# A hybrid attention and feed-forward kernel on Trainium2: other shares of the dequantisation per unit, and the turn of the negated maxima behind the last scores

## The chip, the cores and the metric

The kernel runs on one core of a Trainium2 chip. The core has TensorE (matrix products into PSUM), VectorE, ScalarE and GpSimd (POOL) for work on tiles, and SyncE (SP), which here only issues DMAs. Every engine works off its own list of instructions in order; semaphores make one wait for another. The metric is the device time of one execution in microseconds (us), and less is better. Before the change it is 1792.84 us, the median of three runs (1791.84 to 1794.59).

## The reference

The input x has 2048 tokens of 256 numbers. Four layers are added to it one after the other: attention a, a feed-forward layer, attention b, and the same feed-forward layer again. Each works on a layer-normed x.

```python
x = L0_attn_a_x
x = x + _L0_attn_a_ref(_layernorm(x, axis=-1), ...)
x = x + _L0_ffn_ref(_layernorm(x, axis=-1), ...)
x = x + _L0_attn_b_ref(_layernorm(x, axis=-1), ...)
x = x + _L0_ffn_ref(_layernorm(x, axis=-1), ...)
```

Both attentions are causal, with 16 heads of 16 numbers. Attention a has biases, rotary angles and only 4 key and value heads; attention b has 16 of each and neither biases nor angles.

```python
scores = jnp.einsum('bthd,bshd->bhts', q, k) * scale
scores = jnp.where(causal[None, None, :, :], scores, -jnp.inf)
probs = jax.nn.softmax(scores, axis=-1)
attended = jnp.einsum('bhts,bshd->bthd', probs, v).reshape(B, S, hidden)
return attended @ Wo.T + bo
```

The feed-forward layer has 2048 hidden features. Its three weights come as 4-bit codes with one scale for every 32 of them, and must be dequantised; both feed-forward layers use the same weights.

```python
vals = NVFP4_LUT[idx]
vals = vals.reshape(N, K // block, block) * scales[:, :, None]
...
gelu = jnp.tanh(0.7978845608028654 * (gate + 0.044715 * gate ** 3)) * gate * 0.5 + gate * 0.5
inter = gelu * up
out = jnp.einsum('tn,hn->th', inter, Wd)
```

## The kernel before

**Blocks, groups, units.** The 2048 tokens are cut into four blocks of 512, and the 16 heads into four groups of 4. An attention stage works through 16 units (b, g), block by block, group by group. A unit computes, for 512 queries and 4 heads, the exponentials of all scores up to the diagonal and their products with the values. The number of key tiles grows with the block, so units of block 3 take some 45 to 50 us and those of block 0 some 14 to 24 us.

**What one unit holds.** The row maxima have to be known before the exponentials. So while unit n computes its exponentials, it also computes scores and row maxima of unit n + 1 (`max_steps`): TensorE multiplies (L769, with masks L757), VectorE reduces (L776). After the last of these the step `gather` (L806 to L817, five small VectorE instructions) joins the maxima, negates them and splits them into three bf16 parts in the tile m_pad. The function `turn` (L830) turns m_pad by four matmuls with an identity into a PSUM tile, and ScalarE copies that to the tile mT (L836). In the first five units' turns, four matmuls with zeros (L826) come first. The next unit begins each of its score tiles with a "lift" (L856), two matmuls that write the negated maxima out of mT into PSUM; the scores (L865) are added on top, and ScalarE takes the exponentials (L873). The products of exponentials and values (L911) add up in another PSUM tile.

**The main steps of a unit** (`value_steps`) are a list: two steps for each full key tile, then two for the diagonal squares, two for the first tile of the block, and two that hold both head pairs, `both_pairs(first + 1)` with 256 columns a pair and `both_pairs(first + 2)` with 128. A step is a tuple: its first function is issued, then the side work that falls to it, then the others. The last tuple is `both_pairs(first + 2)` and `rest(0)`, products of an earlier tile (L911 with 384 columns). The product sum is closed, divided and stored inside the first steps of the next unit (`ending`; L942 is the copy of the sum, L949 its turn, L954 and L957 the division).

**The side work of a unit** is woven evenly between the main steps (`weave`), except that the last three (blocks 1 to 3) or two (block 0) get none. It consists of the next unit's maxima, of `out_steps` (the output projection of the block before, L1007) in the first unit of a block, of `prep_steps` (layer norm, projections, rotary angles, keys and queries of the next block) in the first three units of blocks 0 to 2, and, in the first attention only, of the dequantisation. Blocks 1 and 2 put more into their third units: there the first four maxima steps for the next block are computed beside those of the unit that follows.

**The dequantisation** (`dequant_steps`) is a list of 72 steps, six for each of twelve pieces: the load of codes (SP, L330) and of scales (eight DMA issues on POOL, L339), the extraction of the lowest bytes (POOL, L344), two unpackings on VectorE (L355, L357 or L359, and L361; 128 x 128), and two scalings on VectorE (L370; 128 x 512). The load of a piece stands one piece ahead. The first eight pieces go to the gate and up weights in SBUF, the last four by way of DRAM (`wd_kept`) to the down weights. `room` (L1019) gives each unit a weight and `shares` the number of steps that are done by its end, 72 times the running sum over the whole sum, rounded up. The second attention is run with an empty list.

**Order.** All five engines' orders are written out by the program (a manual schedule): an instruction is issued on its engine where the code calls it. PSUM has three tiles ps_s for scores, maxima and the feed-forward features, one tile ps_m for turns and projections, and one ps_av for products. Four tiles hold exponentials.

**The feed-forward stage** runs over the blocks and 16 feature tiles; its first block's layer norm and turning (`beside`) lie in the last attention unit.

The lines that hand the turn to a unit's last step:

```python
if turn:
    scored, summed = steps[-1]
    steps[-1] = (turn, scored, summed)
```

Of the kernel before, what the change touches and what calls it, by code (L numbers as in the profile page):

```python
# [27 lines left out]
NG = NH // 4  # L28
# [3 lines left out]
NB = S // TB  # L32
# [10 lines left out]
def weave(main, side, rest=0):  # L43


    done = 0
    for n, step in enumerate(main):
        first, *second = step if isinstance(step, tuple) else (step,)
        first()
        want = min(len(side), -(-(n + 1) * len(side) // max(1, len(main) - rest)))  # L50
        while done < want:
            side[done]()
            done += 1
        for f in second:
            f()
    while done < len(side):
        side[done]()
        done += 1


def blend(a, b):

    keyed = [((n + 0.5) / len(a), 0, n, f) for n, f in enumerate(a)]
    keyed += [((n + 0.5) / len(b), 1, n, f) for n, f in enumerate(b)]
    return [f for *_, f in sorted(keyed, key=lambda k: k[:3])]


def cut(steps, n):

    while 0 < n < len(steps) and getattr(steps[n - 1], "open", False):  # L70
        n += 1
    return steps[:n], steps[n:]
# [8 lines left out]
def tile_hybrid_layers(  # L81
# [46 lines left out]
    def ps_m():  # L128
        return psum.tile([P, 512], F32, tag="m", name="ps_m")
# [36 lines left out]
    for src, at in ((bq, 0), (bk, D), (bv, D + 64)):  # L166
        n = src.shape[1]
# [243 lines left out]
    class Attention:  # L411
# [601 lines left out]
        def run(self, extra, beside):  # L1013


            units = [(b, g) for b in range(NB) for g in range(NG)]


            room = [0 if n < NG else 9 if n + 1 == len(units) else 2 * (g < 3 or b + 1 == NB)  # L1019
                    for n, (b, g) in enumerate(units)]  # L1020
            shares = [-(-len(extra) * sum(room[: n + 1]) // sum(room)) for n in range(len(units))]
            given, ending, ahead, early = 0, [], [], None

            def zeros():
                pt = ps_m()
                for _ in range(2):
                    nc.tensor.matmul(
                        pt, lhsT=sel[:, 0, :], rhs=nothing, start=True, stop=True
                    )

            for n, (b, g) in enumerate(units):
                lead, more = [], []
                if g == 0 and b > 0:
                    more += self.out_steps(b - 1)
                if g == 0 and b + 1 < NB:
                    ahead = self.prep_steps(b + 1)

                    third = len(ahead) / 3
                    few = [round(third) - (1 if b else 2), round(third) + (1 if b else 2) + 2 * self.first, len(ahead)]
                if g < 3 and b + 1 < NB:  # L1040
                    part, ahead = cut(ahead, few[g])
                    more += part
                if shares[n] > given:
                    more = blend(more, extra[given : shares[n]])
                    given = shares[n]
                if n == 0 and self.after:
                    lead, more = self.after[:3], self.after[3:] + more
                elif n + 2 < len(units):
                    self.load_q(*units[n + 2])
                maxima, turn = [], None  # L1050
                if n + 1 < len(units):
                    maxima, turn = early or self.max_steps(*units[n + 1])
                    early = None
                    if g == 2 and 0 < b < NB - 1:

                        others, then = self.max_steps(b + 1, 0)
                        half = len(maxima) // 2
                        maxima = maxima[:half] + blend(maxima[half:-1], others[:4]) + maxima[-1:]
                        early = others[4:], then
                else:  # L1060
                    more = blend(more, beside)
                steps, end, divide = self.value_steps(b, g)

                for at, step in zip((0, 2), ending):
                    scored, *summed = steps[at]
                    steps[at] = (scored, step, *summed)
                if turn:
                    scored, summed = steps[-1]
                    steps[-1] = (turn, scored, summed)
                if (b, g) == (0, 3):  # L1070

                    maxima = blend(maxima[:-1], [zeros] * 8) + maxima[-1:]
                some, left = (3, 3) if b else (1, 2)
                first = len(maxima) * some // len(steps)
                weave(steps[:some], lead + maxima[:first])
                weave(steps[some:], blend(maxima[first:], more) if maxima else more, rest=left)
                ending = [end, divide]
            end()
            return [divide] + self.out_steps(NB - 1)
# [93 lines left out]
    with tc.tile_pool(name="wk1", bufs=2) as wk, tc.tile_pool(name="kv1", bufs=1) as kv:  # L1173
        at.wk = at.qpool = wk
        with tc.tile_pool(name="init", bufs=1) as pool:
# [14 lines left out]
            steps, turn = at.max_steps(0, 0)  # L1190
# [16 lines left out]
    with tc.tile_pool(name="kv20", bufs=1, reuse_waits="tile") as kv0, tc.tile_pool(  # L1207
# [8 lines left out]
        steps, turn = at.max_steps(0, 0)  # L1216
# [60 lines left out]
```

## Time and profile before

| What | us |
|---|---|
| Median of three runs (lowest, highest) | 1792.84 (1791.84, 1794.59) |
| The profiled execution | 1790.76 |
| Its span, first to last instruction | 1789.0 |
| TensorE busy | 1709.7 (96%) |
| VectorE busy | 1113.2 (62%) |
| ScalarE busy | 799.8 (45%) |
| GpSimd busy | 242.2 (14%) |
| First attention, turn of unit (0,0) to the end of unit (3,3) | 36.3 to 566 |
| Second attention, likewise | 924.2 to 1446 |

All times inside an execution come from one profiled execution and are counted from the start of its span. Line numbers (L830) are those of the kernel before. In a timeline a line gives the start, the duration, the engine, the line, the operation and its tiles (written <- read), the shapes and the number of instructions merged, and in brackets how long the engine stood idle before and which instruction released it. Ends of matmuls are modelled, and neighbours on an engine overlap a little, on ScalarE and VectorE by some 0.1 us. "PEclk" is the clock that TensorE was granted, 1.00 being full. PE is TensorE, PEld its loading of weights, DVE VectorE, ACT ScalarE.

### The profile page before, as it was taken

Reading aid. Unit: us, or ns where it says so; the run is one execution under the profiler, and the core shown is the slowest. Engines: PE = TensorE matmul, PEld = TensorE weight load, DVE = VectorE, ACT = ScalarE, POOL = GpSimd, SP = SyncE. Lnnn points to the kernel's source line nnn. Section 1 sums busy time; section 2 is a strip of 40 time slices with the busy share of each in tenths; the row PEclk is TensorE's granted clock in tenths of the full one; section 3 lists DMA queues with packets and bytes.
Section 4 is the critical chain, followed back from the end, with each engine's and each line's share of the span. In section 5 each row is a group of like instructions: output and inputs, shape, how many; then the busy total and the mean of one; then the engine's idle time right before and its main releaser. Section 6 shows DMA issues by size and latency. Waiting matters only on the chain.

```text
span 1789.0 us, 30446 instructions
## 1 busy us (share of the span) xinstructions
PE 1709.7 (96%) x12814; PEld 934.3 (52%) x12829; DVE 1113.2 (62%) x1615; ACT 799.8 (45%) x1016; POOL 242.2 (14%) x476
## 2 busy tenths in 40 slices
PE   8888899899999999999998899999999999999999
PEld 4544454444443474656475445444444445565646
DVE  5667987887874626362645777777878535445352
ACT  2435556666666313131314455555666742222231
POOL 4312211201103102012101010000000001111010
PEclk9999999999999999999999999999999999999999
DMA  5321301310003000005006042032000100000000
GB/s 154 92 60 56 73 25 46 73 29 25 13 2 125 6 1 1 0 0 129 1 2 129 17 89 50 13 66 54 14 13 1 49 1 3 9 7 6 10 3 12
DMA packets 43129, 65.33 MB, mean 37 GB/s; under 512 B 14000, under 2 KB 21040, under 8 KB 42736
## 3 DMA queue, kind: packets, MB, share of 16 engines
q1 hardware_dynamic: 34352, 47.37, 9.2%
q0 software_dynamic: 7680, 15.48, 4.9%
q8 instruction: 101, 1.65, 0.4%
q10 hardware_dynamic: 960, 0.52, 0.1%
q14 instruction: 36, 0.29, 0.1%
HBM read 43.45 MB, written 17.83 MB: 34 GB/s over the span
## 4 chain that ended last, share of the span: by engine, by line
PE 57%; DVE 7%; ACT 3%; issue 1%; POOL 0%; ACTq 0%; DVEq 0%; POOLq 0%
PE ps_s L1126 24%; PE ps_m L1151 6%; PE ps_av L1151 6%; DVE mx L776 6%; PE ps_av L911 6%; PE ps_s L856 4%; PE ps_s L769 3%; PE ps_s L865 3%; ACT e L873 2%; PE ps_m L1002 1%; PE ps_m L501 1%; PE ps_s L501 1%; PE ps_s L757 1%; PE ps_m L636 0%; PE ps_m L1102 0%
## 5 line engine op out<-in xcount | busy, mean ns | idle before, releaser
L776 DVE TENSOR_REDUCE mx<-ps_s 128x2 f32<-128x1024 f32 (+3 forms) x576 | 650.2, 1160 | 198.2 <-PE ps_s L769 152.0
L873 ACT ACTIVATE e<-ps_s 128x1024 f32<-128x1024 f32 (+1 forms) x576 | 555.6, 977 | 378.4 <-PE ps_s L865 307.1
L911 PE MATMUL ps_av<-e,v 128*32 128x256 f32 (+3 forms) x4672 | 331.9, 376 | 0.1
L865 PE MATMUL ps_s<-qT,kT 64*128 64x512 f32 (+3 forms) x1664 | 329.3, 445 | 0.0
L769 PE MATMUL ps_s<-kT,qT 64*128 64x512 f32 (+3 forms) x1664 | 258.0, 364 | 30.5 <-DVE mx L776 16.2
L1126 PE MATMUL ps_s<-xnT,wg 128*128 128x512 f32 x512 | 240.9, 593 | 0.0
L1126 PE MATMUL ps_s<-xnT,wu 128*128 128x512 f32 x512 | 240.6, 592 | 0.0
L856 PE MATMUL ps_s<-mT,sel 64*128 64x512 bf16 (+3 forms) x1280 | 219.1, 354 | 19.9 <-DVE mx L776 8.4
L769 PEld LDWEIGHTS ps_s<-kT,qT 64*128 64x128 f32 x1664 | 141.8, 186 | 126.0 <-DVE mx L776 53.8
L856 PEld LDWEIGHTS <-sel 64*128 64x128 bf16 x1280 | 66.6, 93 | 230.9 <-issue 218.1
L1132 ACT ACTIVATE t<-ps_s 128x512 f32<-128x512 f32 x128 | 76.3, 596 | 244.2 <-PE ps_s L1126 243.9
L1135 ACT ACTIVATE t<-t 128x512 f32<-128x512 f32 x128 | 80.6, 629 | 198.8 <-DVE t L1134 198.8
L1134 DVE TENSOR_TENSOR t<-ps_s,t 128x512 f32<-128x512 f32 x128 | 88.1, 688 | 124.5 <-POOL t L1133 122.3
L911 PEld LDWEIGHTS ps_av<-e,v 128*32 128x32 f32 x4672 | 102.3, 109 | 113.9 <-issue 99.4
L1126 PEld LDWEIGHTS ps_s<-xnT,wu 128*128 128x128 f32 x512 | 97.3, 190 | 122.5 <-issue 122.5
L1133 POOL TENSOR_SCALAR t<-t 128x512 f32<-128x512 f32 x128 | 79.1, 618 | 534.5 <-ACT t L1132 534.0
L865 PEld LDWEIGHTS ps_s<-qT,kT 64*128 64x128 f32 x1664 | 149.2, 193 | 2.0
L1126 PEld LDWEIGHTS ps_s<-xnT,wg 128*128 128x128 f32 x512 | 95.1, 190 | 104.2 <-issue 102.5
L1136 DVE SCALAR_TENSOR_TENSOR t<-t,ps_s 128x512 f32<-128x512 f32 x128 | 88.1, 688 | 89.0 <-ACT t L1135 89.0
L1151 PE MATMUL ps_av<-wd,inter 128*128 128x256 f32 x512 | 114.4, 380 | 0.0
L1151 PE MATMUL ps_m<-wd,inter 128*128 128x256 f32 x512 | 114.1, 379 | 0.0
L1151 PEld LDWEIGHTS ps_av<-wd,inter 128*128 128x128 f32 x512 | 96.8, 190 | 16.9 <-issue 4.2
(153 smaller groups left out, 1103.5 us busy)
## 6 DMA issues: line engine op xcount, KB each, us to landing
qT<-h SPq DMA_DIRECT2D x248, 64.0 KB, 2.2
kT<-h POOLq DMA_DIRECT2D x88, 128.0 KB, 5.9
h<-high SPq DMA_DIRECT2D x24, 256.0 KB, 2.2
h<-low SPq DMA_DIRECT2D x24, 256.0 KB, 2.5
wd<-wd_kept SPq DMA_DIRECT2D x2, 2048.0 KB, 8.2
wd_kept<-dq_d SPq DMA_DIRECT2D x4, 512.0 KB, 2.7
out<-x SPq DMA_DIRECT2D x16, 128.0 KB, 1.7
x<-x SPq DMA_DIRECT2D x3, 512.0 KB, 7.7
```

What stands on the lines that cost most here:

```text
L769: nc.tensor.matmul(pt[:, r, at : at + keys.stop - keys.start], lhsT=self.qT[b, g][64 * r : 64 * r + 64, p, i * P : (i + 1) * P], rhs=self. ...
L776: nc.vector.tensor_reduce(to, pt, AX.X, ALU.max)
L856: nc.tensor.matmul(pt[:, r, at : at + queries.stop - queries.start], lhsT=sel[64 * r : 64 * r + 64, p, :], rhs=self.mT[b, g][64 * r : 64 * ...
L865: nc.tensor.matmul(pt[:, r, at : at + queries.stop - queries.start], lhsT=self.key_rows(kt // NT, g, p, r, keys), rhs=self.qT[b, g][64 * r ...
L873: nc.scalar.activation(e, pt, AF.Exp, scale=QK_SCALE)
L911: nc.tensor.matmul(held["av"][32 * j : 32 * j + 32, to], lhsT=self.vv[kt // NT][:, kt % NT, h * VW : h * VW + 32], rhs=of(j), start=openin ...
L1126: nc.tensor.matmul(pt[:, k, :], lhsT=w[:, c, fc * P : (fc + 1) * P], rhs=self.xnT[b][:, c, :], start=(c == 0), stop=(c == 1),)
L1133: nc.gpsimd.tensor_scalar(t, t, GELU_A, 1.0, ALU.mult, ALU.add)
L1134: nc.vector.tensor_tensor(t, gate, t, ALU.mult)
L1135: nc.scalar.activation(t, t, AF.Tanh, scale=GELU_C)
L1136: nc.vector.scalar_tensor_tensor(t, t, 1.0, gate, ALU.add, ALU.mult)
L1151: nc.tensor.matmul(po[:, :D], lhsT=inter[:, fc, i * P : (i + 1) * P], rhs=wd[:, fc, :], start=(fc == 0), stop=(fc == NFC - 1),)
```

## The change

The weights in `room` become a written list. The sum stays 27. In steps of the dequantisation, by unit from (0,0) to (3,3): before 0, 0, 0, 0, 6, 5, 5, 0, 6, 5, 5, 0, 6, 5, 5, 24; after 0, 0, 0, 0, 6, 5, 0, 0, 5, 8, 0, 0, 8, 6, 5, 29. The third units of blocks 1 and 2 get none, and the steps keep their order. The first attention alone has such steps.

In the last tuple of a unit, `turn` and `scored` change places, in both attentions and at all units but the last: `both_pairs(first + 2)` is issued first, then the turn with its copy on ScalarE, then `rest(0)`. On TensorE the scores of the last step (L856, L865) come ahead of L830, and on ScalarE the exponentials of that step (L873) ahead of the copy to mT (L836). The number and kind of instructions are the same on every engine. All lines behind L1018 have numbers one less.

```diff
@@ -1016,8 +1016,7 @@
             units = [(b, g) for b in range(NB) for g in range(NG)]
 
 
-            room = [0 if n < NG else 9 if n + 1 == len(units) else 2 * (g < 3 or b + 1 == NB)
-                    for n, (b, g) in enumerate(units)]
+            room = [0, 0, 0, 0, 2, 2, 0, 0, 2, 3, 0, 0, 3, 2, 2, 11]
             shares = [-(-len(extra) * sum(room[: n + 1]) // sum(room)) for n in range(len(units))]
             given, ending, ahead, early = 0, [], [], None
 
@@ -1066,7 +1065,7 @@
                     steps[at] = (scored, step, *summed)
                 if turn:
                     scored, summed = steps[-1]
-                    steps[-1] = (turn, scored, summed)
+                    steps[-1] = (scored, turn, summed)
                 if (b, g) == (0, 3):
 
                     maxima = blend(maxima[:-1], [zeros] * 8) + maxima[-1:]
```

## The prediction

> **What bounds the kernel now.** I read the page first: engine shares, then the chain that ended last.
>
> ```profile
> PE 1709.7 (96%) x12814; PEld 934.3 (52%) x12829; DVE 1113.2 (62%) x1615; ACT 799.8 (45%) x1016; POOL 242.2 (14%) x476
> ...
> PE 57%; DVE 7%; ACT 3%; issue 1%; POOL 0%; ACTq 0%; DVEq 0%; POOLq 0%
> ```
>
> TensorE is nearly always busy, so a microsecond in which it newly waits is lost, unless it would have waited later anyway. The change works in the two attention stages only (36 to 566 us and 924 to 1446 us). Next, the timeline at a boundary between two units; of thirty, fifteen look like this one, which ends unit (3,1) of the second attention. First TensorE, then ScalarE.
>
> ```profile
> 1365.90 0.48 PE L865 MATMUL ps_s<-qT,kT 64*128 64x256 f32 x4
> 1366.31 0.40 PE L830 MATMUL ps_m<-ident_b,m_pad 128*128 128x128 bf16 x4
> ...
> 1366.73 0.42 PE L865 MATMUL ps_s<-qT,kT 64*128 64x128 f32 x4
> 1367.08 0.85 PE L911 MATMUL ps_av<-e,v 128*32 128x384 f32 x8
> 1368.03 0.39 PE L856 MATMUL ps_s<-mT,sel 64*128 64x512 bf16 x2
> ```
>
> ```profile
> 1366.48 1.02 ACT L873 ACTIVATE e<-ps_s 128x1024 f32<-128x1024 f32 x1 [0.56 <-PE ps_s L865]
> 1367.40 0.58 ACT L836 CAST mT<-ps_m 128x512 bf16<-128x512 f32 x1
> 1367.86 0.62 ACT L873 ACTIVATE e<-ps_s 128x512 f32<-128x512 f32 x1
> 1368.75 1.02 ACT L873 ACTIVATE e<-ps_s 128x1024 f32<-128x1024 f32 x1 [0.27 <-PE ps_s L865]
> ```
>
> See the order: turn (L830), last scores (L865, 128 columns), their products, then the next unit's lift (L856), which needs mT. The copy of mT (L836) begins only when ScalarE has finished the exponentials of the step before (1366.48 to 1367.50), ends at 1367.98, and the lift starts 0.05 later; the products had ended at 1367.93. Copy and lift already meet there: the cover is used up.
>
> A few boundaries look otherwise, as the first one of the first attention:
>
> ```profile
> 50.09 0.23 DVE L817 TENSOR_TENSOR m_pad<-rest,m_pad 128x16 bf16<-128x16 f32 x1
> ...
> 50.38 0.40 PE L830 MATMUL ps_m<-ident_b,m_pad 128*128 128x128 bf16 x4 [2.57 <-DVE m_pad L817]
> ```
>
> Here TensorE stands 2.57 us before VectorE's last gather instruction. Last, the units by windows: (1,2), (2,1), (2,2), (3,1) of the first attention, then (3,1) of the second, which has no dequantisation.
>
> ```profile
> 173.55:203.46 29.91, 25.92 (x284) 14.21 (x285) 27.02 (x38) 16.59 (x20) 11.11 (x21) 1.00 0.35 97
> ...
> 269.63:311.17 41.54, 40.05 (x409) 20.07 (x409) 32.01 (x42) 25.88 (x31) 7.23 (x13) 1.00 0.15 48
> 311.17:352.98 41.81, 37.42 (x398) 19.25 (x397) 36.72 (x48) 24.12 (x28) 11.15 (x21) 1.00 0.24 63
> ```
>
> ```profile
> 439.62:485.07 45.45, 44.27 (x490) 20.80 (x489) 38.85 (x45) 30.61 (x32) 4.57 (x9) 1.00 0.08 24
> ```
>
> ```profile
> 1321.32:1366.31 44.99, 44.07 (x490) 21.01 (x489) 36.37 (x37) 30.60 (x32) 0.00 (x0) 1.00 0.05 13
> ```
>
> Columns: length, then busy time of PE, PEld, DVE, ACT, POOL. TensorE idles 3.99 us in (1,2) and 4.39 in (2,2), but 1.49 in (2,1) and 1.18 in (3,1): VectorE holds it up in the third units.
>
> **Part 1, the turn behind the last scores: thirty boundaries.** No instruction is added or taken. On TensorE the scores move ahead of the four turning matmuls; so ScalarE, in its own order, meets the last exponentials (0.62) before the copy (0.58). SP, POOL and VectorE keep their order. At a boundary as shown, the exponentials start where the copy did (1367.40) and the copy 0.52 later (0.62 less the 0.10 by which neighbours on ScalarE overlap). Copy ends 1368.50, lift at 1368.55 instead of 1368.03: 0.52 us. Queued behind the lift on TensorE are the next unit's scores, with them VectorE's next maxima and ScalarE's next exponentials; nothing on TensorE may pass it. Fifteen of these: 15 x 0.52 = 7.8. Four boundaries have ScalarE free earlier (copy 0.63, 0.71, 0.84 and 0.91 us after the turn's start, against 1.09): the same shift there gives 0.22, 0.29, 0.42 and 0.50, together 1.4. Stalls: 9.2.
>
> Where the gather is late, the scores fill the wait. At 50.38 the lift came 1.56 after the turn's start; afterwards only the turn and the products (0.85) precede it, about 1.12: a gain of 0.44. Four such boundaries give 0.44, 0.35, 0.44 and 0.40, one half-late one 0.11, four others (ScalarE free, gather in time) 0.2 in all, one nothing: 1.9. The thirtieth, behind (1,2), goes with part 2. Sum: +7.3. Bounds: nothing absorbed and no late gather gained, +9.2; half of each stall absorbed by the 0.48 us wait for ScalarE that follows in each such unit, +2.7. I take +7.3, because that later wait hangs on the first exponentials and so on the lift, and shifts with it.
>
> **Part 2, the shares.** Cumulative 72 x room / 27, rounded up, gave units (1,0) to (3,3) 6, 5, 5, 0, 6, 5, 5, 0, 6, 5, 5, 24 steps; it becomes 6, 5, 0, 0, 5, 8, 0, 0, 8, 6, 5, 29. The steps themselves cost the same. In (1,2) VectorE ran almost without a gap from 176 to 203 us:
>
> ```profile
> 184.14 0.89 DVE L370 SCALAR_TENSOR_TENSOR wu<-dq_e,dq_s 128x512 f32<-128x512 fp8e4 x1
> ...
> 189.01 0.67 DVE L370 SCALAR_TENSOR_TENSOR wu<-dq_e,dq_s 128x512 f32<-128x512 fp8e4 x1
> ```
>
> With overlaps taken off, these two and one unpacking step cost 0.81 + 0.59 + 0.59 = 2.0 us of its queue. TensorE's waits for VectorE there are 1.11 + 0.22 within and 1.01 at the end, so nearly all comes back at the turn: -1.9. But the exponentials before then end 0.65 after the turn's new start instead of 0.12, the last ones 0.52 later, the copy 0.47 after that: lift at 1.69 instead of 1.55, so -1.7 net. In (2,2) two unpackings and two scalings, 0.6 each, leave: of the first and third nothing is won, as VectorE waits for TensorE behind them (0.41 and 0.46 idle before its next work); of the second and fourth 0.6 each: -1.2. The bound is all 2.0 + 2.4 = -4.4 on one side, on the other the 1.01 alone, -1.0.
>
> Where the steps go: VectorE gets 1.6 us more in (2,1), 0.5 in (3,0), 0.7 in (3,2), 0.6 less in (2,0). Price: block 3 of the second attention does the same work without dequantisation; (3,0) to (3,2) are there 0.87, 0.46 and 0.93 shorter, 2.26 us for 7.28 us of dequantisation, or 0.31 per us. 2.2 x 0.31 = +0.7 (bounds 0 and 2.2). In (3,3) VectorE is busy 13.87 of 35.43 us; five more steps hide there, and the last, at 566.98, has 4.8 us before the feed-forward needs VectorE (571.80). The dequantised weights are needed later still. POOL's scale loads (eight issues, 4.0 us a piece) and SP's loads of packed codes move with the steps, behind query loads for units not yet begun: nothing, but ScalarE's copy of rotated queries in (2,1) may come late behind them, up to 1 us if that cover fails. Sum: 0.7 - 1.7 - 1.2 = -2.2.
>
> **Total** 7.3 - 2.2 = +5.1 us. The profiled execution took 1790.76 (span 1789.0 and 1.76 around it), so 1795.9; the median of three is 1792.84, which gives 1797.9.
>
> **A rule against it.** The clock shows what idling costs:
>
> ```profile
> 100.68:104.09 3.41, 1.55 (x11) 0.82 (x10) 3.38 (x5) 0.81 (x1) 0.00 (x0) 1.00 0.04 11
> 104.09:107.51 3.42, 2.88 (x11) 1.34 (x14) 1.67 (x3) 0.00 (x0) 0.00 (x0) 0.50 0.00 0
> ```
>
> After a stretch with TensorE busy 1.55 of 3.41 us the granted clock was 0.50 for the next. At the boundaries idle time grows from some 0.64 us to 1.2 in such a stretch, busy 2.2; the stretch 199.66 to 203.07, in (1,2), was as idle and 1.00 followed. By the rows: no loss. The Trainium skill (TensorE: Matmul & The Clock Gate, "A second HAM failure mode: psum-queue depth-cycling") says that frequent short idling between groups of matmuls can also make the clock oscillate. An estimate from its halved clock for one 3.4 us window at each of 19 boundaries would be 32 us more; no run here shows that.
>
> **Rivals.**
> - The stall is absorbed (other side): ScalarE's chain, not the lift, starts a unit, and the 19 stalls cost nothing. For it: the 0.48 us wait behind each. Against it: ScalarE idles 0.27 before its first exponentials, waiting for L865. Sum -1.9 - 2.2 = -4.1: 1788.7. The sign turns when a stall costs under 0.23 us.
> - Third units give back all VectorE time (-4.4, and 0 for the steps elsewhere): 7.3 - 4.4 = +2.9, 1795.7; with part of the stalls absorbed too, less. Within the bound.
> - More drops of the clock: each 3.41 us at half speed costs 1.7. Two to four: +3.4 to +6.8, 1801 to 1805. For it: early units already fall (0.50 above); against it, the busy late ones never did.
>
> **How the numbers follow.** Forecast 0.60 (own range 1795 to 1801), absorbed 0.08, all VectorE time returned 0.20, clock 0.12. A measurement tells 0.2%, 3.6 us, from no change: slower from 1796.4. The forecast's lower sixth lies below that, so slower 0.50 + 0.12, same 0.10 + 0.20, faster 0.08. All low bounds together (2.7 - 4.4 + 0) give 1791.1, all high ones (9.2 - 1.0 + 2.2 + 1) 1804.2; that all fall together is unlikely, so the range is 1792 to 1802, which leaves out the absorbed case and most of the clock's.
>
> **What would show it.** Right: the copy of mT starts 1.6 us after the last exponentials but one, the lift waits for it at late boundaries, both attention stages change, the second by about +4.0, the first by about +1. TensorE's idle falls by 1 to 2 us in (1,2) and (2,2). Wrong: the second attention, which has the turn alone, is not longer; or the granted clock falls in new places.

## The result and the profile after

The changed kernel takes 1796.71 us (median of 16 runs, 1791.84 to 1800.73), the kernel before 1791.26 us beside it (16 runs, 1789.56 to 1796.76). The ratio is 1.0030, 95% interval 1.0021 to 1.0039: 5.4 us slower (3.8 to 7.0). Differences in us against the kernel before are the ratio taken on its median, here and below; the difference of the two medians can be some 1 us off them. The profiled executions have spans of 1794.5 and 1789.0 us.

No engine does more work. The first lines of the page of the kernel after:

```profile
span 1794.5 us, 30440 instructions
## 1 busy us (share of the span) xinstructions
PE 1708.9 (95%) x12814; PEld 936.0 (52%) x12829; DVE 1112.1 (62%) x1615; ACT 799.0 (45%) x1016; POOL 242.7 (14%) x476
```

TensorE is busy 0.8 us less over a span that is 5.5 us longer: the time went into waits. The groups by line, asked for the copy to mT, tell which. Under "who waited for it (us, times)" the kernel before and then the kernel after have, for the lift (L856):

```profile
  PE ps_s L856: 1.3, 2
```

```profile
  PE ps_s L856: 15.4, 25
```

The two places before are the first units of the two attentions, and they stay. Waits of 0.10 us, as at the late boundaries before, are under what this view counts.

The boundary that the prediction showed, the end of unit (3,1) of the second attention, in the timeline of the kernel after; TensorE, then ScalarE:

```profile
1370.42 0.48 PE L865 MATMUL ps_s<-qT,kT 64*128 64x256 f32 x4
...
1370.84 0.42 PE L865 MATMUL ps_s<-qT,kT 64*128 64x128 f32 x4
1371.19 0.40 PE L830 MATMUL ps_m<-ident_b,m_pad 128*128 128x128 bf16 x4
1371.52 0.85 PE L911 MATMUL ps_av<-e,v 128*32 128x384 f32 x8
1373.05 0.39 PE L856 MATMUL ps_s<-mT,sel 64*128 64x512 bf16 x2 [0.68 <-ACT mT L836]
```

```profile
1371.01 1.51 ACT L873 ACTIVATE e<-ps_s 128x1024 f32<-128x1024 f32 x2 [0.56 <-PE ps_s L865]
1372.40 0.59 ACT L836 CAST mT<-ps_m 128x512 bf16<-128x512 f32 x1
```

The two exponentials now stand together (1.51 us), the copy starts 0.12 us before they end, and TensorE stands 0.68 us at the lift, where it stood 0.10.

For the units I take the length from lift to lift, out of the same timelines. It has the wait at the unit's end in it; for (3,3) it goes to the first matmul of the feed-forward stage.

| Stretch, us | before | after | difference |
|---|---|---|---|
| First attention, block 0 | 75.84 | 73.31 | -2.53 |
| First attention, (1,0) to (3,2) | 419.08 | 422.08 | +3.00 |
| First attention, (3,3) | 34.43 | 34.43 | 0.00 |
| Second attention, block 0 | 74.00 | 74.35 | +0.35 |
| Second attention, (1,0) to (3,2) | 413.33 | 417.75 | +4.42 |
| Second attention, (3,3) | 33.62 | 33.62 | 0.00 |
| The two feed-forward stages | 701.3 | 701.3 | 0.0 |

Block 0 is a special case. There the granted clock of TensorE falls to 0.50 for one or two stretches of 3.41 us at a time, and where this happens differs between executions (before: from 80.2 and 104.1 us of the span in the first attention; after: from 44.2 and 102.2). In the profiles of this study the first block 0 took 70.4 to 75.8 us. Nothing of the change can be read from one such number, and the other rows are the ones to compare. They add up to 7.4 us, 2.0 more than the two medians show. (What is missing to 5.5 us is the start, ahead of the first unit.)

The units of the shares, by windows of the kernel after: (1,2), (2,1), (2,2), (3,1) of the first attention.

```profile
171.35:199.80 28.45, 25.51 (x284) 14.23 (x285) 25.23 (x33) 15.88 (x20) 6.69 (x12) 1.00 0.38 86
267.18:309.22 42.04, 40.33 (x409) 20.13 (x409) 33.34 (x49) 25.97 (x32) 7.30 (x13) 1.00 0.13 41
309.22:350.83 41.61, 37.51 (x398) 18.96 (x397) 34.15 (x40) 23.89 (x28) 6.70 (x12) 1.00 0.34 72
438.77:485.27 46.50, 44.30 (x490) 21.14 (x489) 38.10 (x45) 30.59 (x33) 4.47 (x10) 1.00 0.10 30
```

VectorE lost 1.8 us of work in (1,2) and 2.6 in (2,2). TensorE's idle time fell in (1,2) from 3.99 to 2.94 us, but in (2,2) only from 4.39 to 4.10; the new stall at the lift lies within each of these. In (3,1), where VectorE has no more to do than before (38.10 against 38.85), idle time rose by 1.0, of which the stall is 0.6.

### The profile page after: what moved, and what is told of

It reads as the page before. It is cut to its first block, busy times and chain, and to the rows that moved or that the text cites. A ratio compares the mean times of both kernels' runs of the same rounds, so it can differ in the third digit from the quotient of the medians.

```text
span 1794.5 us, 30440 instructions
## 1 busy us (share of the span) xinstructions
PE 1708.9 (95%) x12814; PEld 936.0 (52%) x12829; DVE 1112.1 (62%) x1615; ACT 799.0 (45%) x1016; POOL 242.7 (14%) x476
## 4 chain that ended last, share of the span: by engine, by line
PE 74%; DVE 15%; ACT 7%; issue 2%; DMA 1%; POOL 0%; ACTq 0%; SPq 0%; DVEq 0%; POOLq 0%
PE ps_s L1125 24%; DVE mx L776 12%; PE ps_av L911 10%; PE ps_s L856 7%; PE ps_m L1150 6%; PE ps_s L769 6%; PE ps_av L1150 6%; PE ps_s L865 5%; ACT e L873 5%; PE ps_s L501 2%; PE ps_m L1002 2%; PE ps_m L501 1%; PE ps_s L757 1%; ACT mT L836 1%; PE ps_m L949 1%
## 5 line engine op out<-in xcount | busy, mean ns | idle before, releaser
L873 ACT ACTIVATE e<-ps_s 128x1024 f32<-128x1024 f32 (+1 forms) x576 | 552.1, 976 | 384.8 <-PE ps_s L865 314.1
L865 PE MATMUL ps_s<-qT,kT 64*128 64x512 f32 (+3 forms) x1664 | 327.6, 445 | 0.0
L856 PE MATMUL ps_s<-mT,sel 64*128 64x512 bf16 (+3 forms) x1280 | 219.0, 353 | 31.0 <-ACT mT L836 15.4
L856 PEld LDWEIGHTS <-sel 64*128 64x128 bf16 x1280 | 67.1, 93 | 240.1 <-issue 230.2
L865 PEld LDWEIGHTS ps_s<-qT,kT 64*128 64x128 f32 x1664 | 149.4, 193 | 1.9
```

Of the source, the lines that this page charges most:

```text
L856: nc.tensor.matmul(pt[:, r, at : at + queries.stop - queries.start], lhsT=sel[64 * r : 64 * r + 64, p, :], rhs=self.mT[b, g][64 * r : 64 * ...
L865: nc.tensor.matmul(pt[:, r, at : at + queries.stop - queries.start], lhsT=self.key_rows(kt // NT, g, p, r, keys), rhs=self.qT[b, g][64 * r ...
L873: nc.scalar.activation(e, pt, AF.Exp, scale=QK_SCALE)
```

## Experiments

The theory: the last exponentials stand ahead of the copy on ScalarE, the lift waits for the copy, and nothing later takes this up. The main rivals: it is TensorE's own order (too little left behind the turn to cover the copy), whatever ScalarE does; or the stall is taken up later; or the differences are falls of the clock. Each group of runs had its own runs of the kernel before beside it, on the same chip.

**The turn alone.** The shares of before, the order of after.

```diff
-                    steps[-1] = (turn, scored, summed)
+                    steps[-1] = (scored, turn, summed)
```

> The turn behind the last scores, with the shares of before. Theory (the last exponentials stand ahead of the copy of mT on ScalarE, so the lift waits): +6 to +7 us against before, the second attention +4.8 us longer as in the changed kernel, 0.48 us at each late boundary. Rival (where the clock falls in the first units makes the difference, the turn nothing): within 2 us of before, and the late units as long as before. Rival (the stall is absorbed later in a unit): under +2 us.

1797.39 us (6 runs) against 1790.13 (18 runs), ratio 1.0045 (1.0029 to 1.0061): +8.1 us (5.2 to 10.9). Units (1,0) to (3,2) are 3.09 us longer in the first attention and 5.19 in the second, and the lift waits for the copy 15.0 us in 24 places. All of the loss is in this part of the change. The expected 6 to 7 lie within the interval.

**The shares alone.**

```diff
-            room = [0 if n < NG else 9 if n + 1 == len(units) else 2 * (g < 3 or b + 1 == NB)
-                    for n, (b, g) in enumerate(units)]
+            room = [0, 0, 0, 0, 2, 2, 0, 0, 2, 3, 0, 0, 3, 2, 2, 11]
```

> The new shares, with the turn ahead of the last scores as before. Theory: -1 to -2.5 us against before, the second attention unchanged, units (1,2) and (2,2) together 2 to 3 us shorter and the units that got the steps 0.5 to 1.5 us longer. Rival (the third units give back all of VectorE's time, and the steps are free elsewhere): -4.4 us. Rival (the steps cost elsewhere what they cost there): 0.

1788.42 us (12 runs), ratio 0.9991 (0.9982 to 1.0001): -1.6 us (-3.2 to +0.2), not clear of none. The interval leaves out the rival of -4.4 us, but not the rival of 0. Lift to lift, against before: (1,2) -1.49, (2,0) +0.53, (2,1) -0.10, (2,2) -0.58, (3,0) +0.16, (3,1) +0.61, (3,2) +0.05, which is -0.82 in all. The two units that were freed give 2.07 us, the low end of the expected 2 to 3, and 1.25 of it goes again in the other five, within the expected 0.5 to 1.5.

**The copy ahead of the last exponentials.** TensorE as in the changed kernel, shares as in the changed kernel; the exponentials of the last step are issued behind the turn. For this the last step's scores and exponentials become two functions. Of that edit, the lines that set the order:

```diff
-                    scored, summed = steps[-1]
-                    steps[-1] = (scored, turn, summed)
+                    scored, raised, summed = steps[-1]
+                    steps[-1] = (scored, turn, raised, summed)
```

> As the changed kernel on TensorE (scores, then turn), but on ScalarE the copy to mT is issued ahead of the last exponentials. Theory (ScalarE's order is the cause): at the late boundaries the lift waits 0.1 us again and not 0.68, the early boundaries keep their gain; -3 to -4 us against before. Rival (TensorE's order is the cause: behind the turn only 0.85 us of products are left as cover, whatever ScalarE does): +4 to +5.5 us, as the changed kernel, with the lift still waiting 0.5 us or more.

1783.48 us (7 runs), ratio 0.9969 (0.9954 to 0.9984): -5.6 us (-8.2 to -2.9) against before, where the changed kernel loses 5.4. The same boundary, ScalarE and then the lift:

```profile
1360.06 0.58 ACT L836 CAST mT<-ps_m 128x512 bf16<-128x512 f32 x1
1360.53 0.62 ACT L873 ACTIVATE e<-ps_s 128x512 f32<-128x512 f32 x1
```

```profile
1360.70 0.39 PE L856 MATMUL ps_s<-mT,sel 64*128 64x512 bf16 x2 [0.19 <-ACT mT L836]
```

TensorE's order is that of the changed kernel, and the stall is gone but for 0.19 us: the late units have their old length again, within some 0.02 us in most. So it is ScalarE's order, and not TensorE's. The expected 3 to 4 us lie within the interval. In the profiles units (1,0) to (3,2) of both attentions are 3.2 us shorter than before; how much of the rest is the clock in block 0 (72.6 us here, 75.8 before, in the first attention) can't be told.

**VectorE copies.** The changed kernel, with the copy on the engine that is idle at this point.

```diff
-                nc.scalar.copy(self.mT[b, g], pt)
+                nc.vector.tensor_copy(self.mT[b, g], pt)
```

> As the changed kernel, but VectorE, which is idle between the gather and the next unit's maxima, copies the turned maxima to mT. Theory (the copy waits in ScalarE's queue): the copy starts within 0.1 us of the end of the turn, the lift waits at most 0.1 us, and the time is 4 to 5.5 us under that of before. Rival (TensorE's order is the cause): the lift still waits about 0.5 us and the time is +4 to +5.5 us against before.

1782.97 us (6 runs), ratio 0.9961 (0.9946 to 0.9976): -7.0 us (-9.7 to -4.3; expected were 4 to 5.5). The copy takes 0.69 us there instead of 0.58, but it starts at once, and the lift no longer waits at any boundary but the first of each attention. VectorE, then TensorE, at the same boundary:

```profile
1357.40 0.69 DVE L836 CAST mT<-ps_m 128x512 bf16<-128x512 f32 x1 [1.71 <-PE ps_m L830]
```

```profile
1357.29 0.85 PE L911 MATMUL ps_av<-e,v 128*32 128x384 f32 x8
1358.15 0.39 PE L856 MATMUL ps_s<-mT,sel 64*128 64x512 bf16 x2
```

**The shares, once the stall is gone.** The next four ran beside one another: VectorE's copy with the old shares, with the turn ahead again, with (2,0) freed as well, and the kernel of the paragraph before once more.

> VectorE copies the turned maxima, the turn stands behind the last scores, but the shares are those of before. Theory (the shares are worth 1 to 1.6 us by themselves, and add to the rest): 5 to 6 us under before, 1 to 1.6 us over the kernel with VectorE's copy and the new shares. Rival (with the stalls gone the third units' wait at the gather is filled by the last scores, so the new shares bring nothing more): equal to that kernel.

> The kernel with VectorE's copy, the turn behind the last scores and the new shares once more, beside the other three on the same chip: 5 to 8 us under before.

Old shares: 1783.30 us (5 runs), ratio 0.9958 (0.9946 to 0.9970). New shares: 1784.27 us (5 runs), 0.9967 (0.9955 to 0.9979). The times don't show the expected advantage of the new shares, of 1 to 1.6 us; they are spread by the clock of block 0. In the profiles units (1,0) to (3,2) of the first attention are 0.7 us shorter (415.45 against 416.18). The rival's reason, that the last scores now fill the wait in the third units, doesn't hold: (1,2) and (2,2) are 1.48 and 0.50 us shorter with the new shares, as without VectorE's copy. More than half of that goes again in (2,0) and (3,1), 0.52 and 0.69 longer.

> New shares and VectorE's copy, but the turn ahead of the last scores as before. Theory (scores ahead of the turn gain only where the gather is late, some 0.4 us at each of 5 to 9 boundaries; at the late boundaries either order is covered once ScalarE's queue is out of the way): about 2 us over the kernel with VectorE's copy and the turn behind, 4 to 5 us under before, and no wait at the lift in blocks 2 and 3. Rival (the place of the turn matters at every boundary): 5 us or more over that kernel.

```diff
-                    steps[-1] = (scored, turn, summed)
+                    steps[-1] = (turn, scored, summed)
```

1787.05 us (11 runs), ratio 0.9978 (0.9968 to 0.9987), in the medians 2.8 us over the order of after with the same copy; the intervals overlap, and units (1,0) to (3,2) of both attentions are 1.3 us longer. No late lift waits in either order. So what the change does on TensorE is rather a small gain (argued from medians and one profile each), and what it does on ScalarE is the loss.

> As the kernel with VectorE's copy and the new shares, but unit (2,0) gets no dequantisation and (3,3) 34 steps in place of 29. Theory (a step costs where TensorE waits for VectorE, and (2,0) has such waits of 0.6 and 0.8 us): (2,0) 0.5 to 1.2 us shorter, (3,3) the same length, the whole 0.5 to 1.2 us less. Rival (five more steps no longer fit under (3,3), where eight scale loads of a piece take POOL 4 us): the layer norm of the feed-forward comes late and the whole is 0 to 3 us more.

```diff
-            room = [0, 0, 0, 0, 2, 2, 0, 0, 2, 3, 0, 0, 3, 2, 2, 11]
+            room = [0, 0, 0, 0, 2, 2, 0, 0, 0, 3, 0, 0, 3, 2, 2, 13]
```

1791.28 us (12 runs), ratio 1.0001 (0.9988 to 1.0013): 7.0 us over the kernel with 29 steps in (3,3). (2,0) is 1.30 us shorter (39.54 against 40.84), as the theory had it, but (3,3) is 41.48 us long instead of 34.44, which is more than the rival's 0 to 3. Two lines of TensorE's timeline in (3,3), two of VectorE's, and then windows of 3.4 us over it:

```profile
547.25 0.51 PE L1101 MATMUL ps_m<-ident,xn 128*128 128x128 f32 x2 [1.48 <-DVE xn L310]
...
549.64 0.67 PE L1101 MATMUL ps_m<-ident,xn 128*128 128x128 f32 x2 [1.33 <-DVE xn L310]
```

```profile
546.18 0.23 DVE L355 TENSOR_SCALAR dq_t<-dq_b 128x128 uint32<-128x128 uint32 x1 [5.85 <-POOL dq_b L344]
...
546.79 0.41 DVE L310 TENSOR_SCALAR xn<-x,mv,rstd 128x256 f32<-128x256 f32 x1
```

```profile
541.90:545.30 3.40, 3.40 (x32) 0.87 (x28) 0.00 (x0) 3.33 (x4) 3.38 (x7) 1.00 0.20 65
545.30:548.80 3.50, 1.53 (x10) 0.59 (x8) 2.47 (x9) 2.30 (x4) 0.85 (x2) 1.00 0.02 8
548.80:552.20 3.40, 2.56 (x14) 0.61 (x14) 0.69 (x2) 1.01 (x2) 2.73 (x6) 0.50 0.62 205
552.20:555.60 3.40, 2.10 (x10) 0.90 (x10) 1.37 (x7) 1.94 (x2) 1.93 (x4) 0.50 0.30 104
555.60:559.00 3.40, 3.40 (x22) 1.33 (x23) 1.79 (x4) 0.37 (x1) 1.21 (x3) 0.50 0.19 77
```

VectorE, in its order, waits for POOL's byte extraction (5.85 us ahead of an unpacking at 546.18), and the next layer norm's tiles (xn) stand behind it; TensorE waits for these, was busy only 1.53 of 3.50 us, and its clock was 0.50 for the next 10.2 us. It was not so in every execution: one of the twelve took 1784.91 us at a mean granted clock of 0.997, four about 1791 at 0.989. So (3,3) has room for 29 steps and mostly not for 34.

**The best shares found.** (2,0) freed, with eight steps each in (1,0) and (1,1) and 29 in (3,3), beside the old shares once more; VectorE copies in both.

```diff
-            room = [0, 0, 0, 0, 2, 2, 0, 0, 2, 3, 0, 0, 3, 2, 2, 11]
+            room = [0, 0, 0, 0, 3, 3, 0, 0, 0, 3, 0, 0, 3, 2, 2, 11]
```

> VectorE's copy, the turn behind the last scores, and shares that free (2,0) too: the five steps go to (1,0) and (1,1), eight each, and (3,3) keeps 29. Theory (a step costs only where TensorE waits for VectorE): (2,0) 1.3 us shorter as in the run that gave its steps to (3,3), (1,0) and (1,1) together 0 to 0.8 us longer, (3,3) 34.4 us again with no fall of the clock in it; 0.5 to 1.3 us under the kernel with VectorE's copy and the new shares. Rival (a step costs the same wherever it stands before the last unit): no difference.

> The kernel with VectorE's copy, the turn behind the last scores and the shares of before, once more and beside the kernel with the early shares: 6 to 8 us under before.

1780.49 us (6 runs) and 1783.10 us (6 runs) against 1790.23 (11 runs) before: 0.9952 (0.9933 to 0.9970) and 0.9959 (0.9943 to 0.9974). Against the new shares of the change, (2,0) is 1.29 us shorter, (1,1) 0.95 longer, (1,0) the same, (3,3) 34.43 without a fall of the clock; units (1,0) to (3,2) of the first attention are 0.4 us shorter, where 0.5 to 1.3 were expected of the time. This kernel has the lowest time of the study, 8.6 us under before (5.4 to 12.0), though against the old and the new shares the difference isn't settled: the intervals overlap.

**The stall doubled.** The changed kernel, with the copy issued twice.

```diff
-                nc.scalar.copy(self.mT[b, g], pt)
+                for _ in range(2):
+                    nc.scalar.copy(self.mT[b, g], pt)
```

> The changed kernel, with the copy to mT issued twice in a row on ScalarE, so that the wait that the change brought is about doubled. Theory (the lift hangs on ScalarE's queue and nothing later takes the wait up): about 0.47 us more at each of the thirty boundaries, 0.58 less an overlap of some 0.1; 13 to 15 us over the changed kernel, 18 to 20 us over before, the wait at the lift 1.1 to 1.2 us in the late units. Rival (the stalls are absorbed later in the unit): under 8 us over the changed kernel. Rival (short waits make the clock fall): granted clock 0.5 in stretches of blocks 1 to 3 and 25 us or more over before.

1813.72 us (4 runs) against 1790.23, ratio 1.0126 (1.0109 to 1.0144): +22.6 us, some 17 over the changed kernel (17.0 between the profiled spans). The same boundary, ScalarE and then TensorE (line numbers are one higher behind the edit):

```profile
1388.16 1.21 ACT L837 CAST mT<-ps_m 128x512 bf16<-128x512 f32 x2
```

```profile
1389.42 0.39 PE L857 MATMUL ps_s<-mT,sel 64*128 64x512 bf16 x2 [1.29 <-ACT mT L837]
```

The wait goes from 0.68 to 1.29 us. The 22 units (1,0) to (3,2) of both attentions are 12.9 us longer than in the changed kernel, 0.59 each: the added wait goes into the unit's length in full. The second copy cost 0.61 and not 0.47: in the trace it waits for a semaphore that the first one sets and starts 0.03 us behind the first one's end, so there is no overlap. That is enough for the miss in the total. The clock stayed at 1.00 in blocks 1 to 3.

## Why the prediction was right

The forecast was +5.1 us, 1797.9 us; measured were +5.4 and 1796.71. The second attention was forecast about 4.0 us longer and the first about 1; in the profiles they are 4.8 and 0.5.

*Part 1, the late boundaries* (9.2 us of stalls, 0.52 at each of fifteen): as it was worked out. The copy starts where the exponentials let it, the lift waits 0.68 instead of 0.10 us, and the turn alone lengthens units (1,0) to (3,2) by 3.09 and 5.19 us, where the boundaries of these units sum to some 3.3 and 5.4 in the working (the first with the gain of 0.4 behind (1,2), which the text put with part 2). One sign was misreckoned: the copy starts 1.39 us after the start of the last exponentials but one, not 1.6; the prediction's own times (1367.40 + 0.52, less 1366.48) make it 1.44. That nothing takes the stall up later, which was argued from the first exponentials hanging on the lift, is shown by the doubled copy. The cause, ScalarE's order, is shown by putting the copy ahead again.

*The early boundaries* (a gain of 0.44 where the gather is late): where ScalarE was free, at the ends of (0,0) of the first attention and of (0,1) and (0,3) of the second, the lift came 1.11 to 1.14 us after the turn's start, where 1.12 was worked out. At the ends of (1,0) and (1,1) of the first, where TensorE had waited 0.73 and 0.61 us for the gather, the copy came behind the last exponentials and the lift 1.42 and 1.53 us after the turn; these units changed by no more than 0.1 us. What the early gains are worth in the time is covered by the clock of block 0, which the prediction counted with nothing in its sum.

*Part 2, the shares* (-2.2): right in sign, too large. (1,2) gave 1.49 us by itself for the 1.9 expected, (2,2) 0.58 for 1.2. The term that was most off is "+0.7" for the units that take the steps: by one price per microsecond of dequantisation, (2,0), with less of it, should have gained 0.2 and (3,1), with the same amount, should have stayed. They lost 0.53 and 0.61, and the five units together 1.25. By the timelines of the shares alone, TensorE's waits for VectorE go from 1.93 to 2.27 us in (2,0) and from 0.27 to 0.54 in (3,1). That the steps fall beside other maxima there is the likely reason, not a shown one, and the rest of the 0.53 and 0.61 isn't settled. That an amount doesn't tell the price is seen in the last shares too: five steps less gave 1.29 us in (2,0), three more cost 0.95 in (1,1), and two more nothing in (1,0). With this the shares' units sum to -0.8 under the old order of the turn, and under the new one to -0.1 (422.08 against 422.17 for the turn alone).

*The total* was nearer than its parts, and that is luck: in the profiles, the shares gave 1.4 to 2.1 us less than was forecast, and block 0 of the first attention was 2.5 us shorter, which the sum did not hold; the clock fell elsewhere in it. The other runs say the same. The nine runs of the changed kernel with a mean granted clock of 0.995 have a median of 1796.94 us (1795.44 to 1799.05), the ten of the kernel before beside the experiments with that clock 1789.41 (1789.10 to 1791.57): 7.5 us, near the 7.4 of units (1,0) to (3,2), though the chips may differ. So by these runs the change costs, at an equal clock, about 2 us more than was forecast, and most of that is what the shares did not give.

*The rivals.* "Absorbed" is refuted by the doubled copy, "all VectorE time returned" by the shares alone. "More drops of the clock" did not happen: all falls in the changed kernel's attentions lie in block 0. The rule of the Trainium skill that was set against it (TensorE: Matmul & The Clock Gate, "A second HAM failure mode: psum-queue depth-cycling") was estimated at 32 us; with stalls of 0.68 us, and even of 1.29 us, at the late boundaries the granted clock stayed 1.00 in blocks 1 to 3. What comes nearest to it is unit (3,3) with 34 steps: there no single wait was over 1.5 us, and the clock halved all the same. The prediction's own ground for no loss, one stretch as idle that was followed by 1.00, does not carry that far, as the last section shows.

## What to carry to other kernels

When a step is moved on one engine, write down what it issues on the others: here the move seems harmless, rather good, on TensorE, and the loss lay in the order of two instructions on ScalarE. At a hand-over that everything waits for, the short copy goes first in its queue, or to an engine that is idle there, even if the copy itself is slower on it (0.69 against 0.58 us). Side work that is moved for balance has to be looked at where it lands, instruction by instruction; amounts per unit mislead by as much as they promise.

## What was not expected of the hardware

The clock of TensorE fell where short waits added up: busy 1.53 of 3.50 us, with a wait of 1.48 and the beginning of one of 1.33, stood ahead of 10.2 us at half speed, and five more side steps cost 7.0 us. But neither the busy share of a stretch of 3.41 us nor its longest wait tells whether the clock falls after it. In the kernel before, this stretch has no wait over 0.89 us, and the clock was 0.50 from its end on:

```profile
76.78:80.19 3.41, 2.52 (x19) 1.57 (x19) 2.36 (x4) 1.90 (x3) 0.00 (x0) 1.00 0.21 77
```

The stretch from 46.06, busy 1.59 us, in which the wait of 2.57 begins that the prediction shows, was followed by 1.00, and so was that from 199.66, busy 2.15. What tells them apart stays open here.
